# Storing 128 output rows at a time in 43.8 KB packets instead of 8 KB packets for four tiles together

## The chip, the cores and the metric

The kernel runs on one core of a Trainium2 chip. The metric is device time in microseconds (us), the median of several executions. The kernel before takes 1312.68 us (1312.46 to 1312.87 in 3 runs). Engines are named as in the profile: DVE is VectorE, ACT ScalarE, POOL GpSimd, PE TensorE, SP SyncE, which issues the transfers. "DMA engine" means one of the sixteen engines that move data; "q1" is the queue with the kernel's transfers.

## The reference

Each of 4096 rows of 256 numbers is multiplied with itself as an outer product, of which the upper triangle is kept, row by row:

```python
def reference(r_inputs):                      # (4096, 256) float32
    dot = jnp.einsum('bi,bj->bij', r_inputs, r_inputs)
    iu, ju = jnp.triu_indices(256)
    return dot[:, iu, ju]                     # (4096, 32896) float32
```

4.19 MB come in and 538.97 MB go out, with one multiplication per output value. It is a problem of storing.

## The kernel before

Batch rows lie on the 128 partitions. Four batch tiles (512 rows) are computed together. An output row is cut into 16 chunks of 2,048 or 2,176 columns, and each chunk of four tiles leaves in one store. In it every partition contributes four contiguous runs of 8 KB, and each run is one packet (the record has 65,536 store packets, of 8,192 or 8,704 bytes).

```python
CHUNKS = 16     # pieces that an output row is cut into
GROUP = 4       # batch tiles of 128 rows that are computed and stored together
SHORT = 64      # runs up to this length take one instruction for the whole group
...
opool = ctx.enter_context(tc.tile_pool(name="o", bufs=4))
...
for g in range(groups):
    for c, (lo, hi) in enumerate(zip(borders, borders[1:])):
        o = opool.tile([P, GROUP, widest], F32, tag="o", name=f"o_{g}_{c}")
        for i, j, col, length in runs(d, lo, hi):       # x[i] * x[j : j + length]
            a = col - lo
            if length <= SHORT:
                nc.vector.tensor_tensor(...)             # all four tiles
                continue
            for t in range(GROUP):
                ...
                if t == GROUP - 1:
                    nc.scalar.activation(dst, src, AF.Copy, scale=factor)
                else:
                    nc.vector.tensor_scalar(dst, src, factor, None, ALU.mult)
        nc.sync.dma_start(x_out[g][:, :, lo:hi], o[:, :, : hi - lo])
```

Of the kernel before, what the change touches and what calls it, by code (L numbers as in the profile page):

```python
# [1 line left out]

# [4 lines left out]

F32 = mybir.dt.float32
AF = mybir.ActivationFunctionType
ALU = mybir.AluOpType  # L10

P = 128
UNIT = 128      # columns: chunk borders are multiples of it, 512 bytes in HBM
CHUNKS = 16     # pieces that an output row is cut into
GROUP = 4       # batch tiles of 128 rows that are computed and stored together
SHORT = 64      # runs up to this length take one instruction for the whole group


def chunk_borders(width: int) -> list[int]:
    units = width // UNIT  # L20
    borders = [units * c // CHUNKS * UNIT for c in range(CHUNKS)]
    return borders + [width]


def runs(d: int, lo: int, hi: int):
    """The runs of output columns [lo, hi) with one first factor: (i, j, column, length), for
    x[i] * x[j : j + length]. Row i of the upper triangle has j from i on."""
    at = 0
    for i in range(d):
        a, b = max(at, lo), min(at + d - i, hi)  # L30
        if a < b:
            yield i, i + a - at, a, b - a
        at += d - i


@with_exitstack
def kernel(
    ctx: ExitStack, tc: tile.TileContext, x: bass.AP, out: bass.AP
):
    """out[n, :] = the upper triangle, row by row, of the outer product of x[n] with itself.  # L40

    Batch rows lie on the partitions. The input stays on chip; the output is made chunk by chunk
    and each chunk goes out in one store while the next ones are computed."""
    nc = tc.nc
    n, d = x.shape
    width = out.shape[1]
    assert n % (P * GROUP) == 0 and width == d * (d + 1) // 2 and width % UNIT == 0
    groups = n // (P * GROUP)
    borders = chunk_borders(width)
    widest = max(b - a for a, b in zip(borders, borders[1:]))  # L50

    xpool = ctx.enter_context(tc.tile_pool(name="x", bufs=1))
    opool = ctx.enter_context(tc.tile_pool(name="o", bufs=4))

    x_in = x.rearrange("(g t p) d -> g p t d", t=GROUP, p=P)
    x_out = out.rearrange("(g t p) c -> g p t c", t=GROUP, p=P)

    xs = []
    for g in range(groups):
        xt = xpool.tile([P, GROUP, d], F32, tag=f"x{g}", name=f"x{g}")  # L60
        nc.sync.dma_start(xt, x_in[g])
        xs.append(xt)

    for g in range(groups):
        xt = xs[g]
        for c, (lo, hi) in enumerate(zip(borders, borders[1:])):
            o = opool.tile([P, GROUP, widest], F32, tag="o", name=f"o_{g}_{c}")
            for i, j, col, length in runs(d, lo, hi):
                a = col - lo
                if length <= SHORT:  # L70
                    nc.vector.tensor_tensor(  # L71
                        o[:, :, a : a + length],
                        xt[:, :, j : j + length],
                        xt[:, :, i : i + 1].to_broadcast([P, GROUP, length]),
                        ALU.mult,
                    )
                    continue
                for t in range(GROUP):
                    dst = o[:, t, a : a + length]
                    src = xt[:, t, j : j + length]  # L80
                    factor = xt[:, t, i : i + 1]
                    # Of four such instructions one goes to the Scalar engine.
                    if t == GROUP - 1:
                        nc.scalar.activation(dst, src, AF.Copy, scale=factor)  # L84
                    else:
                        nc.vector.tensor_scalar(dst, src, factor, None, ALU.mult)  # L86
            nc.sync.dma_start(x_out[g][:, :, lo:hi], o[:, :, : hi - lo])  # L87


# [1 line left out]
_INS = ["r_inputs"]  # L91
_OUTS = [((4096, 32896), "float32")]


# [20 lines left out]
```

## Time and profile before

| | before |
|---|---|
| median time | 1312.68 us |
| profiled span | 1310.8 us |
| VectorE busy | 1116.7 us, 5,272 instructions |
| ScalarE busy | 504.8 us, 1,553 instructions |
| q1's packets, share of sixteen DMA engines | 71,808, 100.0% |
| plateau of the transfer rate | 419 to 420 GB/s |
| instruction fetches (queue 14) in the span | 57 packets |

The prediction below prints the lines of the page. Read them for one thing: which row has no room left? A compute engine with a high busy share that waits for the transfers (here VectorE: 85% busy, 167 us of waits for stores) does not bound the kernel.

The trace keeps sixteen completion marks for each transfer (2,176 for the 136 of this kernel), and a store is called landed here at its last one. I take each mark for that of one DMA engine; the stage table of the changed kernel below bears this out, with 2.9, 1.8 and 1.1 engines at work where three, two and one marks are still to come. The prediction gives the marks of the last store: the end is set by one DMA engine that finishes almost 10 us after the others.

### The profile page before, as it was taken

Reading aid. Unit: us, or ns where it says so; the run is one execution under the profiler, and the core shown is the slowest. Engines: PE = TensorE matmul, PEld = TensorE weight load, DVE = VectorE, ACT = ScalarE, POOL = GpSimd, SP = SyncE. Lnnn points to the kernel's source line nnn. Section 1 sums busy time; section 2 is a strip of 40 time slices with the busy share of each in tenths; the row PEclk is TensorE's granted clock in tenths of the full one; section 3 lists DMA queues with packets and bytes.
Section 4 is the critical chain, followed back from the end, with each engine's and each line's share of the span. In section 5 each row is a group of like instructions: output and inputs, shape, how many; then the busy total and the mean of one; then the engine's idle time right before and its main releaser. Section 6 shows DMA issues by size and latency. Waiting matters only on the chain.

```text
span 1310.8 us, 7383 instructions
## 1 busy us (share of the span) xinstructions
DVE 1116.7 (85%) x5272; ACT 504.8 (39%) x1553; POOL 0.2 (0%) x4
## 2 busy tenths in 40 slices
DVE  8889977899778997789977899778996789967893
ACT  5345234442344423345333443334433443334430
POOL 0000000000000000000000000000000000000000
DMA  9999999999999999999999999999999999999996
GB/s 370 428 428 421 420 419 419 419 420 419 419 419 419 420 419 420 419 419 419 419 420 419 419 419 419 419 418 419 420 419 419 419 419 418 420 419 419 419 419 274
DMA packets 71865, 543.64 MB, mean 415 GB/s; under 512 B 2176, under 2 KB 6272, under 8 KB 6272
## 3 DMA queue, kind: packets, MB, share of 16 engines
q1 hardware_dynamic: 71808, 543.17, 100.0%
q14 instruction: 57, 0.47, 0.1%
HBM read 4.19 MB, written 538.97 MB: 414 GB/s over the span
## 4 chain that ended last, share of the span: by engine, by line
DMA 54%; DVE 43%; issue 0%; DVEq 0%; SPq 0%
DMA out_dram<-o 54%; DVE o L86 34%; DVE o L71 9%; DMA x<-in_r_inputs_dram 0%; DVEq L71 0%; DVEq L86 0%; SPq L87 0%; DVEq L111 0%
## 5 line engine op out<-in xcount | busy, mean ns | idle before, releaser
L86 DVE TENSOR_SCALAR o<-x 128x256 f32<-128x256 f32 (+44 forms) x4656 | 989.7, 291 | 111.4 <-DMA out_dram<-o 106.9
L84 ACT ACTIVATE o<-x 128x105 f32<-128x105 f32 (+59 forms) x1552 | 503.5, 411 | 764.4 <-DMA out_dram<-o 762.0
L71 DVE TENSOR_TENSOR o<-x 128x112 f32<-128x112 f32 (+51 forms) x616 | 137.1, 284 | 60.0 <-DMA out_dram<-o 60.0
L84 ACT ACT_TABLE_LOAD x1 | 1.3, 1283 | 0.7 <-PEq L102 0.7
L102 POOL MEMSET const-bfloat16-1.0<- 128x1 bf16 x1 | 0.1, 102 | 0.0
L102 POOL MEMSET const-uint8-127<- 128x1 uint8 x1 | 0.1, 101 | 0.0
L102 POOL MEMSET const-float32-0.0<- 128x1 f32 x1 | 0.1, 98 | 0.2 <-issue 0.2
L102 POOL MEMSET const-float32-1.0<- 128x1 f32 x1 | 0.1, 98 | 0.0
## 6 DMA issues: line engine op xcount, KB each, us to landing
out_dram<-o SPq DMA_DIRECT2D x120, 4096.0 KB, 31.5
out_dram<-o SPq DMA_DIRECT2D x8, 4352.0 KB, 22.6
x<-in_r_inputs_dram SPq DMA_DIRECT2D x8, 512.0 KB, 8.6
```

Source lines behind the costliest of these rows:

```text
L71: nc.vector.tensor_tensor(o[:, :, a : a + length], xt[:, :, j : j + length], xt[:, :, i : i + 1].to_broadcast([P, GROUP, length]), ALU.mult,)
L84: nc.scalar.activation(dst, src, AF.Copy, scale=factor)
L86: nc.vector.tensor_scalar(dst, src, factor, None, ALU.mult)
L102: nc = _bacc.Bacc("TRN2", target_bir_lowering=False, num_devices=1)
```

## The change

The intent is fewer and longer packets. One batch tile is computed at a time. Its 32,896 columns leave in three pieces, each contiguous in a partition and in HBM, so that a partition's share of a store is one packet of 43.8 KB. Every product row takes one instruction, given to whichever of VectorE and ScalarE would finish it sooner by a small cost formula. The first piece is cut in four so that storing starts early. The diff, cut to its core:

```diff
-CHUNKS = 16     # pieces that an output row is cut into
-GROUP = 4       # batch tiles of 128 rows that are computed and stored together
-SHORT = 64      # runs up to this length take one instruction for the whole group
+class Shares:
...
+    def multiply(self, dst, src, factor, length: int):
+        v = self.vector + 130 + 0.51 * length
+        s = self.scalar + 187 + 0.83 * length
+        if v <= s:
+            self.vector = v
+            self.nc.vector.tensor_scalar(dst, src, factor, None, ALU.mult)
+        else:
+            self.scalar = s
+            self.nc.scalar.activation(dst, src, AF.Copy, scale=factor)
+
+REPEAT = 1
+PIECES = 3
+FIRST = [1024, 3072, 7168]
...
+    cuts = sorted({0, 1, groups // 8, groups // 2, groups})
+    for a, b in zip(cuts, cuts[1:]):
+        if a < b:
+            nc.sync.dma_start(xt[:, a:b], x_in[:, a:b])
...
-            o = opool.tile([P, GROUP, widest], F32, tag="o", name=f"o_{g}_{c}")
+            o = opool.tile([P, slot], F32, tag="o", name=f"o_{g}_{c}")
+            cuts = [lo, *FIRST, hi] if g == c == 0 else [lo, hi]
+            for a, b in zip(cuts, cuts[1:]):
+                shares.even()
+                for row, i, j, at, length in runs(d, a, b):
+                    shares.multiply(...)
-            nc.sync.dma_start(x_out[g][:, :, lo:hi], o[:, :, : hi - lo])
+                nc.sync.dma_start(x_out[g][:, a:b], o[:, a - lo : b - lo])
```

More of the change, by code (lines that the diff above doesn't have):

```diff
@@ L12, with even_borders, __init__, even @@
 P = 128
-UNIT = 128
-CHUNKS = 16
-GROUP = 4
-SHORT = 64
-def chunk_borders(width: int) -> list[int]:
-    units = width // UNIT
-    borders = [units * c // CHUNKS * UNIT for c in range(CHUNKS)]
-    return borders + [width]
-def runs(d: int, lo: int, hi: int):
-    at = 0
-    for i in range(d):
-        a, b = max(at, lo), min(at + d - i, hi)
-        if a < b:
-            yield i, i + a - at, a, b - a
-        at += d - i
+UNIT = 64
+def even_borders(lo: int, hi: int, pieces: int) -> list[int]:
+    units = (hi - lo) // UNIT
+    return [lo + units * c // pieces * UNIT for c in range(pieces)] + [hi]
+def runs(d: int, lo: int, hi: int):
+    width = d * (d + 1) // 2
+    for row in range(lo // width, (hi + width - 1) // width):
+        at = row * width
+        for i in range(d):
+            a, b = max(at, lo), min(at + d - i, hi)
+            if a < b:
+                yield row, i, i + a - at, a, b - a
+            at += d - i
+class Shares:
+    def __init__(self, nc):
+        self.nc = nc
+        self.vector = self.scalar = 0.0
+    def even(self):
+        self.vector = self.scalar = 0.0
+    def multiply(self, dst, src, factor, length: int):
[10 more added lines that the diff above has]
+FIRST = [1024, 3072, 7168]
 @with_exitstack
@@ L46 @@
     width = out.shape[1]
-    assert n % (P * GROUP) == 0 and width == d * (d + 1) // 2 and width % UNIT == 0
-    groups = n // (P * GROUP)
-    borders = chunk_borders(width)
-    widest = max(b - a for a, b in zip(borders, borders[1:]))
+    assert n % (P * REPEAT) == 0 and width == d * (d + 1) // 2
+    groups = n // (P * REPEAT)
+    total = REPEAT * width
+    assert total % UNIT == 0
+    borders = even_borders(0, total, PIECES)
+    slot = max(b - a for a, b in zip(borders, borders[1:]))
@@ L52 @@
     xpool = ctx.enter_context(tc.tile_pool(name="x", bufs=1))
     opool = ctx.enter_context(tc.tile_pool(name="o", bufs=4))
-    x_in = x.rearrange("(g t p) d -> g p t d", t=GROUP, p=P)
-    x_out = out.rearrange("(g t p) c -> g p t c", t=GROUP, p=P)
-    xs = []
-    for g in range(groups):
-        xt = xpool.tile([P, GROUP, d], F32, tag=f"x{g}", name=f"x{g}")
-        nc.sync.dma_start(xt, x_in[g])
-        xs.append(xt)
-    for g in range(groups):
-        xt = xs[g]
-        for c, (lo, hi) in enumerate(zip(borders, borders[1:])):
-            o = opool.tile([P, GROUP, widest], F32, tag="o", name=f"o_{g}_{c}")
-            for i, j, col, length in runs(d, lo, hi):
-                a = col - lo
-                if length <= SHORT:
-                    nc.vector.tensor_tensor(
-                        o[:, :, a : a + length],
-                        xt[:, :, j : j + length],
-                        xt[:, :, i : i + 1].to_broadcast([P, GROUP, length]),
-                        ALU.mult,
-                    )
-                    continue
-                for t in range(GROUP):
-                    dst = o[:, t, a : a + length]
-                    src = xt[:, t, j : j + length]
-                    factor = xt[:, t, i : i + 1]
-                    if t == GROUP - 1:
-                        nc.scalar.activation(dst, src, AF.Copy, scale=factor)
-                    else:
-                        nc.vector.tensor_scalar(dst, src, factor, None, ALU.mult)
-            nc.sync.dma_start(x_out[g][:, :, lo:hi], o[:, :, : hi - lo])
@@ new lines @@
+    x_in = x.rearrange("(g p r) d -> p g r d", p=P, r=REPEAT)
+    x_out = out.rearrange("(g p r) c -> g p (r c)", p=P, r=REPEAT)
+    xt = xpool.tile([P, groups, REPEAT, d], F32, name="x")
+    cuts = sorted({0, 1, groups // 8, groups // 2, groups})
+    for a, b in zip(cuts, cuts[1:]):
+        if a < b:
+            nc.sync.dma_start(xt[:, a:b], x_in[:, a:b])
+    shares = Shares(nc)
+    for g in range(groups):
+        for c, (lo, hi) in enumerate(zip(borders, borders[1:])):
+            o = opool.tile([P, slot], F32, tag="o", name=f"o_{g}_{c}")
[3 more added lines that the diff above has]
+                for row, i, j, at, length in runs(d, a, b):
+                    shares.multiply(
+                        o[:, at - lo : at - lo + length],
+                        xt[:, g, row, j : j + length],
+                        xt[:, g, row, i : i + 1],
+                        length,
+                    )
+                nc.sync.dma_start(x_out[g][:, a:b], o[:, a - lo : b - lo])
```

## The prediction

> **What bounds the kernel now.** I read the page first: span, engines, transfer rows. The metric's median is 1312.68 us, the profiled span 1310.8, so an unprofiled time is about 1.9 us above a span.
>
> ```profile
> span 1310.8 us, 7383 instructions
> ...
> DVE 1116.7 (85%) x5272; ACT 504.8 (39%) x1553; POOL 0.2 (0%) x4
> ...
> DMA  9999999999999999999999999999999999999996
> GB/s 370 428 428 421 420 419 419 419 420 419 419 419 419 420 419 420 419 419 419 419 420 419 419 419 419 419 418 419 420 419 419 419 419 418 420 419 419 419 419 274
> DMA packets 71865, 543.64 MB, mean 415 GB/s; under 512 B 2176, under 2 KB 6272, under 8 KB 6272
> ...
> q1 hardware_dynamic: 71808, 543.17, 100.0%
> q14 instruction: 57, 0.47, 0.1%
> HBM read 4.19 MB, written 538.97 MB: 414 GB/s over the span
> ```
>
> VectorE is busy 85%, but the DMA row never leaves 9 before the last slice, and the packets of the one data queue took 100.0% of sixteen engines' span. The rate is flat at 419 to 420 GB/s, after a stretch of 428. The waits say the same from the other side:
>
> ```profile
> ACT o L84 <- DMA out_dram<-o: 762.0, 124, 10.3
> DVE o L86 <- DMA out_dram<-o: 106.9, 46, 3.9
> DVE o L71 <- DMA out_dram<-o: 60.0, 35, 3.4
> ```
>
> Both compute engines wait for stores to free a buffer (VectorE 167 us, ScalarE 762 us in total). So compute is ahead and the stores set the time. The chain of waits gives VectorE 43% of the span; I don't take that for a bound, because a chain that can pass back through either side of a full ring of buffers alternates between them, and no slice shows the transfers short of work.
>
> Next the stages. In the stage table the columns are stretch, length, busy time of VectorE, ScalarE and GpSimd with counts, clock, DMA share and GB/s:
>
> ```profile
> 4.00:12.00 8.00, 7.63 (x30) 7.63 (x21) 0.00 (x0) 1.00 1.03 343
> 30.00:90.00 60.00, 52.28 (x235) 24.42 (x73) 0.00 (x0) 1.00 1.01 428
> 200.00:320.00 120.00, 106.42 (x524) 47.86 (x154) 0.00 (x0) 1.00 1.01 419
> 1299.00:1309.00 10.00, 0.00 (x0) 0.00 (x0) 0.00 (x0) 1.00 0.13 57
> ```
>
> First row: the input, in 1,024-byte packets, moves at 343 GB/s. Second and third: 8,192-byte store packets, first clean, then a little slower. Last: only 0.13 of sixteen engines is busy in the final 10 us, which is two engines at most: one engine finishes late. The completion marks of the last store agree: fourteen engines land between 1299.99 and 1300.25 us, one at 1301.91, one at 1309.95.
>
> From the DMA records themselves I took the duration of single packets: 1,024 bytes 46 ns (median), 8,192 bytes 309 ns in the clean stretch (the median over the whole run is 314), 8,704 bytes 329 ns (lower quartile; 326 is the least). A line through the first two has slope (309 - 46) / 7168 = 0.0367 ns per byte, that is 27.25 GB/s an engine, and 46 - 1024 x 0.0367 = 8.4 ns left over per packet. It gives 328 ns for 8,704 bytes, which fits. This fixed part is what the change can remove.
>
> [...]
>
> ```profile
> L86 DVE TENSOR_SCALAR o<-x 128x256 f32<-128x256 f32 (+44 forms) x4656 | 989.7, 291 | 111.4 <-DMA out_dram<-o 106.9
> L84 ACT ACTIVATE o<-x 128x105 f32<-128x105 f32 (+59 forms) x1552 | 503.5, 411 | 764.4 <-DMA out_dram<-o 762.0
> ```
>
> The mean length of these runs is 158.8 columns (30,816 columns with runs over 64, in 194 pieces per output row). Busy time over count is 212.6 ns on VectorE and 324.4 ns on ScalarE (the means of 291 and 411 include the overlap with the neighbour). The weights in the changed kernel, 130 + 0.51 L and 187 + 0.83 L, give 211 and 319. Good to 2%.
>
> **The change, part by part.**
>
> *Store packets.* Before: 4,096 rows x 16 pieces = 65,536 packets, 4,096 per engine (3,840 of 8,192 bytes, 256 of 8,704). Undisturbed that is 3,840 x 309 + 256 x 328 = 1270.5 us per engine. After: pieces of 10,944, 10,944 and 11,008 columns, 43,776 or 44,032 bytes, each one packet if nothing splits it. By the line, 46 + 42,752 x 0.0367 = 1615 ns and 1624 ns. An engine has 8 partitions x 32 tiles x (2 x 1615 + 1624) = 1242.6 us, plus 24 extra packets from cutting the first store in four (0.2 us). Removed: 27.7 us. In other words some 3,300 packets an engine fewer, at 8.4 ns each.
>
> *Disturbance.* The fourteen ordinary engines start storing at 13.9 us and land at 1300.0: 1286.1 us, which is 15.6 above undisturbed, or 3.8 ns a packet. After about 105 us the packets jitter among the engines (309 becomes 314). Whether this goes with packets or with bytes the trace can't say, as both store sizes are alike. By packet it would be 768 x 3.8 = 3 us after the change, by byte 15.3. I take the middle, 9.
>
> *The late engine.* It is 2.4 us behind when the input is in and 9.9 at the end. It loses 7.5 us over the span; 57 instruction fetches fit, about 50 of them after the start, 0.15 us each, if they all fall on one engine (a guess; the records don't name it). The changed kernel has 4,962 multiplications on VectorE and 3,299 on ScalarE, 8,261 against 6,824, so some 11 fetches of 128 instructions more: 61 x 0.15 = 9.2 us. With the 2.4 at the start, 11.6 instead of 9.9.
>
> *Compute.* By the weights VectorE has 970 us of work and ScalarE 961, per store 7.2, 8.3 and 14.8 us, against 12.9 us for a store to leave (8 x 1.615). Only the third piece is slower than its store, and three pieces need 30.3 us against 38.8. With four buffers, a piece that is begun when a store lands has up to three stores (38 us) queued ahead. The dropped grouped TENSOR_TENSOR instructions (137 us) come back as single ones, but all beside the transfers.
>
> *Start and end.* The input still takes the same 1,024-byte packets, about 12 us, issued ahead of the stores. The first store (1,024 columns) needs only a few instructions and waits in line, as now. The first store packet today starts at 13.9 us, before the input's last packet on the late engine (16.2), so nothing is won there. Compute is far ahead of the queue at the end, so a larger last store costs no tail. From the last landing to the end of the span is 0.8 us.
>
> Sum: 13.9 + 1242.8 + 9 + 11.6 + 0.8 = 1278.1 us span; with 1.9, 1280 us. I say 1281.
>
> **Rivals.** (1) *Bytes, not packets, set the rate*: a ceiling on the HBM side at 419. For it: the plateau is flat. Against: 428 held for some 70 us with the same packets, and 1,024-byte packets show the same fixed 8 ns. Then the time would be 1310 to 1316. (2) *Compute becomes the bound*, through more instructions or the uneven third piece: 85% now falls to 970 / 1278 = 76%. Against it is the slack above. If the weights were 30% low, the time would be about 1290 to 1310. (3) *Disturbance disappears* with long streams, or the fixed cost is larger in the disturbed stage: some 1270. (4) *Disturbance grows with bytes, and each fetch costs its full 0.31 us*: 1278 + 6 + 10 + 2 = 1296.
>
> **Range and chances.** The fixed cost per packet is well measured, so the centre rests on 27.7 us; disturbance gives -6 to +6, the fetches -3 to +10. Range 1270 to 1292. The 2% line is at 1312.68 x 0.98 = 1286.4, inside the range and 5 us above the centre: faster 0.74, within 2% 0.25, slower 0.01.
>
> **What would show it.** The plateau should be at 428 to 433 GB/s, the data packets 12,672 for the stores (32 x 3 x 128 and 384 of the cut first store) besides 4,096 for input, each store packet at least 1615 ns, DMA still 9 in every slice, VectorE and ScalarE each near 960 us busy, with waits for stores of some 250 us each. One engine should still land last, about 10 us late. I am wrong if a store packet takes over 1660 ns (rival 1), if the DMA row has holes that end with VectorE or ScalarE (rival 2), or if 43.8 KB pieces are split into smaller packets.

Where a cut is marked in the text above, a paragraph of figures that no trace of this case shows is taken out. No term of the sum is cut: it stays at 13.9 + 1242.8 + 9 + 11.6 + 0.8 = 1278.1 us, 1280 with the 1.9, each term from the trace or an estimate from it. The two rows behind the cut check the weights in the changed kernel's code: 211 and 319 ns against 212.6 and 324.4 measured.

## The result, and the profile after

The changed kernel takes 1289.94 us (1289.85 to 1289.99, 4 runs), the kernel before 1312.78 beside it. The ratio is 0.9827, with a 95% interval of 0.9813 to 0.9841. Ratios in this document are the mean time of one kernel's fast runs over that of the other's of the same rounds, so not quite the ratio of the medians. The gain of 22.8 us is far outside the noise. It lies in the predicted range, 9 us above its centre.

The page of the changed kernel:

```profile
span 1288.1 us, 8696 instructions
...
DVE 978.5 (76%) x4961; ACT 964.5 (75%) x3299; POOL 0.2 (0%) x4
...
DMA  9999999999999999999999999999999999999992
GB/s 375 430 433 436 436 434 434 435 432 429 429 432 432 433 436 435 433 435 432 420 433 435 434 435 429 423 434 436 432 432 432 423 435 421 431 432 419 416 433 127
DMA packets 18485, 543.73 MB, mean 422 GB/s; under 512 B 1648, under 2 KB 5744, under 8 KB 5872
...
q1 hardware_dynamic: 18416, 543.17, 98.1%
q14 instruction: 69, 0.57, 0.1%
```

The plateau has risen from 419 to some 432 GB/s, and no slice but the last falls below nine tenths. So the packets do what was expected of them. The last slice is worse than before, though: 127 GB/s instead of 274. Both slices are about 32 us long.

Who waits for whom (us in total, times, longest):

```profile
ACT o L52 <- DMA out_dram<-o: 283.6, 59, 5.4
DVE o L49 <- DMA out_dram<-o: 268.3, 59, 5.3
```

Both compute engines now share the work and still wait for buffers. The stores set the time, as before.

Stages of the changed kernel (stretch, length, busy time of DVE, ACT and POOL with counts, clock, DMA share, GB/s):

```profile
200.00:320.00 120.00, 91.78 (x465) 90.31 (x309) 0.00 (x0) 1.00 1.00 432
1266.00:1270.00 4.00, 0.00 (x0) 0.00 (x0) 0.00 (x0) 1.00 0.18 77
1273.00:1278.00 5.00, 0.00 (x0) 0.00 (x0) 0.00 (x0) 1.00 0.11 46
1280.00:1286.00 6.00, 0.00 (x0) 0.00 (x0) 0.00 (x0) 1.00 0.07 29
```

The DMA share times sixteen is the number of DMA engines at work: 2.9, 1.8 and 1.1 in the last three rows. So three engines still work after 1266 us, then two, then one. The completion marks of the last store say when each finishes:

```
us from the span's start        thirteen engines   then     then     then
before (fourteen: 1300.0-1300.3)                            1301.91  1309.95
after                           1263.99-1264.16    1271.22  1278.92  1287.17
```

The ordinary engines gained 36 us. The end gained 22.7, because the latest engine is 23.1 us behind them instead of 9.9. Here lies what is missing from the expected gain. Single packets of 43,776 bytes took 1618 ns (median) and those of 44,032 bytes 1627 ns, against 1615 and 1624 predicted.

The lag does not appear at the end. Below, the lag of the three latest engines behind the median engine, for single stores in the course of the changed kernel's span, with the 8 KB fetches of queue 14 counted from the beginning of the record:

```
store lands at (median)   lags, us            fetches so far
  92.7                    0.81  1.53  2.98     11
 325.6                    3.26  5.28  8.14     24
 636.4                    6.94 10.76 15.42     41
 948.2                    8.80 14.57 21.66     57
1264.1                    7.14 14.84 23.09     74
```

It rises evenly with time, and stops rising at about 23 us. There the ordinary engines are held back: a buffer comes free only when the latest engine has stored its part (60 of VectorE's 61 stops of over 1 us and 59 of ScalarE's 60 end within 60 ns after the last of a transfer's sixteen marks), and filling it takes up to 15 us of the 38.8 us that three queued stores last (38.8 - 15 = 24, an estimate from the store packets' durations and the 14.8 us that the prediction's weights give the third piece). From then on everybody goes at the pace of the latest engine.

### The profile page after: what moved, and what is told of

Its sections match the earlier page's. It is cut to its first block, busy times and chain, and to the rows that moved or that the text cites. A ratio compares the mean times of both kernels' runs of the same rounds, so it can differ in the third digit from the quotient of the medians.

```text
span 1288.1 us, 8696 instructions
## 1 busy us (share of the span) xinstructions
DVE 978.5 (76%) x4961; ACT 964.5 (75%) x3299; POOL 0.2 (0%) x4
## 3 DMA queue, kind: packets, MB, share of 16 engines
q1 hardware_dynamic: 18416, 543.17, 98.1%
## 4 chain that ended last, share of the span: by engine, by line
DMA 68%; DVE 28%; issue 0%; DVEq 0%; SPq 0%
DMA out_dram<-o 68%; DVE o L49 28%; DMA x<-in_r_inputs_dram 0%; DVEq L49 0%; SPq L104 0%; DVEq L128 0%
## 5 line engine op out<-in xcount | busy, mean ns | idle before, releaser
L49 DVE TENSOR_SCALAR o<-x 128x256 f32<-128x256 f32 (+62 forms) x4961 | 978.5, 290 | 271.2 <-DMA out_dram<-o 268.3
L52 ACT ACTIVATE o<-x 128x255 f32<-128x255 f32 (+62 forms) x3298 | 963.2, 386 | 284.4 <-DMA out_dram<-o 283.6
```

Of the source, the lines that this page charges most:

```text
L49: self.nc.vector.tensor_scalar(dst, src, factor, None, ALU.mult)
L52: self.nc.scalar.activation(dst, src, AF.Copy, scale=factor)
```

## The experiments

The question is what makes three DMA engines late. A fetch is a packet that the profile books under "instruction"; there is about one per 128 instructions (57 for 7,383 in the kernel before, 69 for 8,696 in the changed one). My theory is that instruction fetches (queue 14) pass through particular DMA engines and take time there from the store packets, more of it when the packets are long. The first rival is that some engines are simply slower with long packets, whatever the instructions. The costs per fetch in the expectations below are estimates of mine: 0.6 us fits the changed kernel's lag of 23.1 us over some 39 fetches for VectorE's 4,961 instructions, 0.3 us fits 12.0 us over some 41 for its 5,249 with 8 KB packets; for 0.4 and 0.9 I gave no sum. Each of these kernels but one had 4 runs of its own, beside 7 of the kernel before.

### Stores of the change, few instructions

```diff
+                if g == 0:
...                                            # the first batch tile: rows and store as in the change
+                    continue
+                # Wrong on purpose: the same number of values written, by wide instructions.
...
+                nc.vector.tensor_scalar(
+                    o[:, a - lo : split - lo], flat[:, : split - a], xt[:, g, 0, 0:1], None, ALU.mult
+                )
+                nc.scalar.activation(
+                    o[:, split - lo : b - lo], flat[:, : b - split], AF.Copy, scale=xt[:, g, 0, 0:1]
+                )
```

> The changed kernel with its stores untouched; from the second batch tile on, each piece is filled by one wide instruction on VectorE and one on ScalarE (wrong values on purpose): 252 and 200 instructions instead of 4,961 and 3,299. Theory (instruction fetches hold single DMA engines up): without the fetches no engine falls behind, the sixteen completion marks of the last store lie within 3 us, and the time is that of today's ordinary engines, 1264 + 0.9 + 1.9 = 1267 us. Rival (three DMA engines are slower by themselves with 43.8 KB packets): the marks spread over 23 us as before, time 1290 us.

Measured: 1264.10 us, ratio 0.9630; wrong values. The rows of the page for queues 1 and 14:

```profile
span 1262.3 us, 886 instructions
...
q1 hardware_dynamic: 18416, 543.17, 100.0%
q14 instruction: 7, 0.06, 0.0%
```

The same 18,416 packets now fill 100.0% of the sixteen engines' span instead of 98.1%, and the sixteen marks of the last store lie between 1259.8 and 1261.4 us. No engine is late. The rival that some engines are slow with long packets falls: their packets are unchanged here. The ordinary engines end at 1260.5 us, 3.6 earlier than in the changed kernel, where they are held back. Measured from this free pace the latest engine of the changed kernel loses 1287.2 - 1260.5 = 26.7 us.

### Stores of the kernel before, few instructions

The same edit in the kernel before, from the second group on: wide instructions of up to 1,024 columns instead of single rows.

> The kernel before with its stores untouched (8 KB packets), filled by wide instructions from the second group on (wrong values on purpose). Theory (fetches): the last mark comes with the others at 1300 to 1302 us, time 1303 us; with the first run of this set this leaves the packet size alone, worth 36 us. Rival (a slow engine whatever the instructions): 1312 us.

Measured: 1304.37 us, ratio 0.9937. The latest marks are 1.2, 2.4 and 3.1 us behind (ordinary 1298.6). With the first run this makes a table of two factors:

| median us | many instructions | few instructions | lost to instructions |
|---|---|---|---|
| 8 KB packets | 1312.64 (the kernel before) | 1304.37 | 8.3 |
| 43.8 KB packets | 1289.94 (the change) | 1264.10 | 25.8 |
| gained by long packets | 22.7 | 40.3 | |

Long packets are worth 40.3 us. Of these 17.5 are given back, because the instructions cost 25.8 us between long packets instead of 8.3.

### Compute of the change, packets of the kernel before

```diff
-UNIT = 64
+UNIT = 128
-PIECES = 3
-FIRST = [1024, 3072, 7168]
+PIECES = 16
+FIRST = [1024]
-    opool = ctx.enter_context(tc.tile_pool(name="o", bufs=4))
+    opool = ctx.enter_context(tc.tile_pool(name="o", bufs=20))
```

> The changed kernel's compute with the packets of the kernel before: one batch tile at a time in 16 pieces of 8 KB per partition, 20 buffers, correct values, 5,249 and 3,425 instructions. Theory: the ordinary engines end near 1300 us (8 KB packets), the latest about 10 us behind, although there are more fetches than in the changed kernel, because a fetch costs less between short packets: time 1310 to 1314 us. If a fetch costs an engine the same whatever the packets (0.6 us), the latest engine is 25 us behind and the time is about 1325 us. Rival (the gain came from the order of compute or from the start, not the packets): 1290 us.

Measured: 1312.59 us, ratio 1.0000, correct. The new order of compute and the new start bring nothing by themselves; the whole gain belongs to the packets. The ordinary engines land at 1298.1 us, the three late ones 6.6, 8.5 and 12.0 us behind. With 84 fetches in the span, more than the changed kernel's 69, the latest lag is 12.0 us instead of 26.7. So the lag that a fetch leaves behind depends on the packets that surround it; the packet records, read in the section on the prediction, show in what way.

### More instructions on an idle engine

```diff
+    for _ in range(EXTRA):      # 4000; nothing waits for them
+        nc.tensor.matmul(ps[:1, :1], z[:, 0:1], z[:, 1:2], start=True, stop=True)
```

> The changed kernel plus 4,000 weight loads and 4,000 one-element matmuls on TensorE, which is idle otherwise and which nothing waits for: some 62 fetches more. Theory (each instruction stream is fetched through one DMA engine): a further engine falls behind by 62 x 0.6 = 37 us, past the present last one (23 us), or the same engine falls further; time about 1303 us. Rival (slow engines): 1290 us. If the fetches were spread over all engines it would be about 1292 us.

Measured: 1298.48 us, ratio 0.9892, correct: 8.5 us slower than the changed kernel. Neither of my two figures, 1303 or 1292, holds. Engines and queues of this run:

```profile
PE 104.3 (8%) x4000; PEld 101.7 (8%) x4000; DVE 978.3 (75%) x4961; ACT 964.7 (74%) x3299; POOL 0.3 (0%) x5
...
q1 hardware_dynamic: 18416, 543.17, 97.7%
q8 instruction: 31, 0.51, 0.1%
q14 instruction: 69, 0.57, 0.1%
```

TensorE's instructions come through a queue of their own, q8, in 31 packets of 16 KB. Each took about 1 us in the record, all of them before 209 us. They do not fall on one engine: by 253 us five engines were 5.1 to 5.8 us ahead of the median, one 2.8 and one 1.2, while eight lay within 0.8 us and the latest 15.9 behind. At the end the latest engine is again 23.4 us behind the others, now at 1272.5, which is near the limit of 24 us estimated above from the buffers. So instructions that share no data, no buffer and no wait with the stores slow the kernel, here by 8.5 us. That their fetches do it and not their arithmetic is my reading; this run does not separate the two.

### Only one engine with many instructions

In both kernels one engine keeps its single rows from the second batch tile on, and the other fills the rest of the piece by one wide instruction.

```diff
+            if mine != KEEP:
+                continue                    # this row is left to the wide instruction
...
+        if KEEP == "vector":
+            nc.scalar.activation(dst, src, AF.Copy, scale=f)
+        else:
+            nc.vector.tensor_scalar(dst, src, f, None, ALU.mult)
```

With `KEEP = "scalar"`:

> The changed kernel's stores; from the second batch tile on ScalarE keeps its single rows (3,299 instructions) and VectorE fills the rest of each piece by one wide instruction (wrong on purpose). Theory A (each engine's instruction stream is fetched through DMA engines of its own; VectorE's hold up the last one, ScalarE's the one before): the last mark is some 15 to 17 us behind the ordinary ones, time 1264 + 16 = 1280 us. Theory B (all fetches are dealt over the same three DMA engines): the lag goes with the total count, 26 x 0.4 = 10 us, time 1275 us.

With `KEEP = "vector"`:

> The mirror image: VectorE keeps its 4,961 single rows, ScalarE fills the rest by wide instructions (wrong on purpose). Theory A: the last DMA engine is as late as in the changed kernel, time 1288 to 1290 us. Theory B: 26 x 0.6 = 16 us of lag, time 1280 us.

Measured: 1273.20 us (0.9698) with ScalarE's rows and 1289.96 us (0.9826) with VectorE's. The first has these rows on its page:

```profile
span 1271.4 us, 3985 instructions
...
DVE 373.0 (29%) x249; ACT 964.5 (76%) x3299; POOL 0.2 (0%) x4
...
q14 instruction: 32, 0.26, 0.0%
```

and the second these:

```profile
span 1288.1 us, 5597 instructions
...
DVE 978.4 (76%) x4961; ACT 393.3 (31%) x199; POOL 0.2 (0%) x4
...
q14 instruction: 44, 0.36, 0.1%
```

Dropping ScalarE's 3,100 instructions changes nothing (1289.96 against 1289.94). Dropping VectorE's saves 16.7 us. So VectorE's stream alone sets the end of the changed kernel. The marks show how the streams fall on the engines: VectorE's alone makes two engines late, by 23.1 and 6.8 us; ScalarE's alone two, by 10.2 and 7.2. Theory A holds in kind; its 15 to 17 us for ScalarE was too much, and that run lies nearer to the 1275 us of theory B, which the other run rules out. The records do not name the DMA engine of a fetch, but packets of one engine can be strung together (how, see the section on the prediction): with VectorE's rows alone all 11 fetches between 900 and 1270 us stand in the string of the latest engine. What makes the second engine late is not shown.

### Which engines are late

```diff
+                counts = (15, 14, 12, 8, 7, 4, 2)
+                m = b - len(counts) * UNIT
+                nc.sync.dma_start(x_out[g][:, a:m], o[:, a - lo : m - lo])     # the last piece, less 7 slices
+                ... # then slice n from the first counts[n] partitions, and the rest of each slice
```

> The changed kernel with 7 slices of 64 columns of the last piece stored apart, from the first 15, 14, 12, 8, 7, 4 and 2 partitions. [...] No theory about the time, which may be a few us longer for the small transfers at the end.

Measured (one look, state unknown): 1293.9 us, correct. What is cut from the expectation is an assumption on the engines' numbers that no run shows. The store on the first k partitions shows k completion marks, k being 15, 14, 12, 8, 7, 4 and 2, besides one mark at the moment of issue. Ordinary engines report near 1264 us, the late ones near 1271, 1279 and 1287. The stores on 15, 14, 12, 8 and 7 partitions each show all three late marks (the one on 7: four at 1264, then 1271.6, 1279.1 and 1287.7). The store on 4 shows two ordinary marks, 1271.7 and 1287.9. The store on 2 could only be issued at 1274.4 us, and landed within 1.1 us of it, so it waited for neither of the two latest engines. The records do not give a DMA engine's number. If one partition is always served by the same engine in these seven stores, which was not shown, the late engines are those of three of the first seven partitions: the latest that of the third or fourth, the second-latest that of one of the fifth to seventh. A store on the first k partitions cannot leave out just these.

### Packets of half the length

```diff
-PIECES = 3
-FIRST = [1024, 3072, 7168]
+PIECES = 6
+FIRST = [1024, 3072]
-    opool = ctx.enter_context(tc.tile_pool(name="o", bufs=4))
+    opool = ctx.enter_context(tc.tile_pool(name="o", bufs=8))
```

> The changed kernel with 6 pieces of 21.9 KB per partition and 8 buffers: as many instructions, packets of half the length. By the fixed cost per packet the ordinary engines end 768 x 8.4 ns = 6.5 us later, at 1270 us. If the cost of a fetch grows with the packets it waits between (0.3 us at 8 KB, 0.9 at 43.8 KB, so about 0.6), the last engine is 16 to 18 us behind instead of 23 and the time is 1287 to 1290 us. If the cost of a fetch does not depend on the packets, the lag stays 23 us and the time is 1296 us.

Measured: 1292.13 us, ratio 0.9843, correct: between my two figures. The ordinary engines land at 1268.9 us (8.4 above the free pace of long packets, where the fixed cost per packet gave 6.5), the latest 20.5 us behind. The lag of the latest engine grows with the packet, but slower than in proportion: 12.0, 20.5 and 26.7 us at 8, 21.9 and 43.8 KB. Halving the packet saves 6.2 us of lag and costs 8.4 us elsewhere, so of the three lengths the longest is best with these instructions.

### Dealing the instructions by number

If VectorE's number of instructions sets the end, the rows should be dealt so that no stream is long. The short half of a piece's rows goes to ScalarE, the long half to VectorE:

```diff
+        rows = sorted(rows, key=lambda r: r[4])                    # by length
...
+        self.of = {r[3]: "pool" if k < pool else "scalar" if k < scalar else "vector" for k, r in enumerate(rows)}
...
+        if at is not None:            # from the second batch tile on; the first is dealt by time
+            who = self.of[at]
...
```

> The changed kernel with the rows of a piece dealt by number: the shorter half to ScalarE, the longer to VectorE (4,124 and 4,136 instructions instead of 4,961 and 3,299), correct values. If the last DMA engine is held up by VectorE's instruction stream in proportion, its work past the free pace (26.7 us) falls to 26.7 x 4124 / 4961 = 22.2 us, and the time to 1264.1 + 22.2 - 0.9 = 1285.4 us. ScalarE then has some 35 us of work per tile against 38.8 us of stores, so it should not become the bound. If the lag goes with the total count of instructions, which is unchanged, 1290 us.

Measured: 1284.53 us, ratio 0.9786 (interval 0.9772 to 0.9801, "unclear" by the 2% line), correct. The latest lag is 21.5 us (22.2 expected), with the ordinary engines at the free pace of 1260.5. The total number of instructions is the same as in the change, 8,696, so it is VectorE's number that counts and not the total. That it is the longest stream as such is not shown: ScalarE's is as long here (4,136), and its 3,299 rows alone made an engine only 10.2 us late.

A third stream is the next step: the 40 shortest rows of each tile's last piece go to GpSimd.

> Three instruction streams: the 40 shortest rows of a tile's last piece go to GpSimd, of the others 53% (the shorter) to ScalarE, the long ones to VectorE: 3,349, 3,671 and some 1,240 instructions, correct values. By the same proportion the last DMA engine's lag is 26.7 x 3349 / 4961 = 18.0 us and the time 1281 us, if GpSimd's instructions and their fetches cost nothing else. Rival: GpSimd and VectorE hold each other up, or GpSimd is slow enough to leave the stores waiting: 1290 us or more.

Measured: 1281.75 us, ratio 0.9765, correct. This beats both kernels: 30.9 us under the kernel before, 8.2 under the change.

```profile
span 1280.2 us, 8850 instructions
...
DVE 749.5 (59%) x3349; ACT 1075.9 (84%) x3671; POOL 478.0 (37%) x1244
...
q14 instruction: 69, 0.57, 0.1%
```

There are as many fetches on queue 14 as in the change, and GpSimd does not hold the stores up. The latest lag is 18.9 us (18.0 expected), the next ones 16.4 and 12.0.

Summary of the marks of the last store, all in us:

```
                     median engine   third-latest  second-latest  latest     time
before                   1300.1          0.2           1.8          9.9      1312.7
after                    1264.1          7.1          14.8         23.1      1289.9
long, few                1260.5          0.9           0.9          0.9      1264.1
8 KB, few                1298.6          1.2           2.4          3.1      1304.4
8 KB, many               1298.1          6.6           8.5         12.0      1312.6
TensorE added            1272.5          0.3          14.7         23.4      1298.5
ScalarE's rows           1260.3          1.3           7.2         10.2      1273.2
VectorE's rows           1264.1          0.1           6.8         23.1      1290.0
half length              1268.9          8.4          15.8         20.5      1292.1
dealt by number          1260.5         15.3          18.2         21.5      1284.5
with GpSimd              1260.4         12.0          16.4         18.9      1281.8
```

## Why the prediction was right or wrong

The time fell in the range, and the main mechanism held; the forecast of "faster by over 2%" did not come, by 0.3% of the time. The difference between the predicted span of 1278.1 us and the measured 1288.1 splits cleanly.

- **Bound.** Stores set the time before and after. Shown by the DMA row, the waits, and the run with 8 KB packets and new compute, which has the old time.
- **Fixed cost per packet.** Right. The line through 1,024 and 8,192 bytes gave 1615 and 1624 ns for the long packets, and they took 1618 and 1627. An engine's packets at these medians are 8 x 32 x (2 x 1618 + 1627) = 1244.9 us against 1242.6.
- **Disturbance.** "I take the middle, 9": 5.3 us too much. In the run with few instructions the engines start to store at 14.0 us and end at 1260.5. That is 1246.5 us, 3.7 above the 1242.8 of the prediction, near the 3 us that "by packet" gave. In the changed kernel, where ordinary engines are held back, they end at 1264.1 instead of the 1265.7 of the sum: the two misses nearly cancel, which is luck. What the disturbance is was not settled.
- **The late engine.** This term was mis-sized: 11.6 us were predicted, 23.1 came. That is 11.5 too much, and with -1.6 from the ordinary engines and 0.1 from the end it makes up the 10.0 us. Of the 11.6 us, 2.4 were for the start, where the latest engine is in fact 0.7 us behind; the fetches' own term, 9.2, came to 22.4, beyond its margin of +10. The failing step is "0.15 us each, if they all fall on one engine". The 0.15 us was a net figure, read between 8 KB packets and carried over to packets five times as long. The runs show that the lag grows with the packets (12.0, 20.5, 26.7 us) and that three engines fall behind. The number of additional fetches, 12 (69 against 57), was as predicted (11).
- **What a fetch costs.** The packet records show why the net figure could not be carried over. The next packet of a DMA engine starts 3 to 4 ns before the recorded end of the one before, so most packets can be strung together. Between 30 and 1230 us 63 of the changed kernel's 64 fetches have such a successor, and all 53 of the kernel before. A store packet behind a fetch is longer than undisturbed (the lower tenth of its size), in two groups:

| packets | 8 KB (before) | 21.9 KB | 43.8 KB (the change) |
|---|---|---|---|
| median of a fetch's own packet, ns | 309 | 309 | 309 |
| store packet behind it, larger group, longer by | 346 | 378 | 430 |
| the same, smaller group | 112 | 116 | 166 |

  The single-stream runs tell the groups apart: 432 ns (36 of 40 fetches) with VectorE's rows, 168 ns (24 of 28) with ScalarE's; that the order is the same at 8 and 21.9 KB is assumed. So a VectorE fetch takes 0.65 us from its engine between 8 KB packets and 0.74 us between 43.8 KB ones, almost the same. The difference lies afterwards. The 23 packets that follow are on average only 2.0 ns over their undisturbed time at 8 KB, where store packets in general (without those right behind a fetch) are 6.2 over it; at 43.8 KB it is 1.6 against 4.7. If that holds until the next fetch, a late engine regains some 17 us over 4,096 short packets and only 2 us over 768 long ones. As an estimate, the 38 and 39 fetches of the larger group give 38 x 0.65 - 17 = 8 us net before and 39 x 0.74 - 2 = 27 us after; measured were 7.5 and 26.0 (26.7 less 0.7 at the start). So, by this estimate, long packets hardly make a fetch dearer; they leave the engine few packets on which to catch up.
- **Compute.** Right: 978.5 and 964.5 us busy against 970 and 961, waits of 268 and 284 us against "some 250". The uneven third piece never starved the stores (no slice of the DMA row but the last is below 9).
- **Start and end.** Right: the first store packet came at 14.1 us (13.9 before), the last landing 0.9 us before the end of the span.
- **Rivals.** (1), a ceiling at 419 GB/s, falls with the plateau of 432. (2) does not occur. (3) comes closest for the ordinary engines, which alone would have ended near 1264 us. (4) named the right term for the wrong reason: 0.31 us is the fetch's own packet, and the loss is larger; its disturbance by bytes (6 us more) did not come.

What remains open is why the store packet behind a fetch takes longer, and what makes the second-latest engine late. In the changed kernel the strings of the latest and the third-latest engine hold all nine fetches between 1097 and 1270 us (five and four), so the second-latest took none of them. Yet its 62 packets from 1163 to 1265 us took 24 ns longer than undisturbed on average; the lengthening stops at 1252 us, shortly after the last multiplication (1249.7).

## What to carry to other kernels

When transfers are the bound, look past the mean share of the DMA row at the sixteen completion marks of the last store: a late engine can eat a third or more of a gain that the packets have really brought (here 17.5 of 40.3 us). Long packets pay by a fixed cost each (here 8.4 ns), but the instruction streams share the DMA engines with them (here a 43.8 KB store packet behind a fetch took 166 or 430 ns longer), so the number of instructions of one stream (here VectorE's: with 249 instead of 4,961 instructions the time fell from 1289.9 to 1273.2 us) can set the end even though its engine is idle a quarter of the time. Deal instructions by number as well as by time when the compute engines have room (here 1289.9 to 1284.5 us, and 1281.8 with GpSimd).
